# Four pieces of W1's upper blocks issued from ScalarE's queue instead of SyncE's

## The chip, the cores and the metric

The kernel runs on one core of one Trainium2 chip. The metric is the device time of one execution in microseconds (us). TensorE, VectorE, ScalarE, GpSimd and SyncE are called PE, DVE, ACT, POOL and SP where the profile does so.

## The reference, cut to what matters

Two LoRA layers with residuals are applied one after the other to an x of 8 x 256 x 1024 in float32:

```python
# layer 0: adapter chosen per sample by itok_B_0_2
x = x + (x @ W0.T + ((x @ A0[idx0]) @ B0.T) * 0.5)
# layer 1: adapter chosen per sample by itok_B_0_23
x = x + (x @ W1.T + b1 + ((x @ A1[idx1]) @ B1[idx1]) * 2.0)
```

W0 and W1 are 1024 x 1024; A0 has rank 32 and A1, B1 have rank 16.

## The kernel before, in words

Both layers are linear, so the kernel first forms a fused matrix M from (I + W0) and (I + W1), plus small fused adapters, and then multiplies the samples by M in pairs. All products of 512 x 512 blocks use seven-product schemes of the Strassen family, nested, so nearly every product needs operand sums that VectorE makes beforehand.

The order on each engine is written out by hand: the lines of the kernel body run in program order on every engine, and nothing is rescheduled. DMA transfers that SyncE and ScalarE issue share eight completion semaphores, handed round in turn; an issue that takes a semaphore over first waits for the transfer that had it before. So each of these engines' queues can wait at a DMA issue, and whatever stands behind it on that engine waits too.

The stage that the change touches is the first 45 us:

- Loads. W1 is read as four blocks of 512 x 512, block (h, i) being rows 512h to 512h+511 and columns 512i to 512i+511. `load_w1` (L163 to L171) reads a block in four pieces g = 0 to 3, each piece into 32 partitions (32g to 32g+31), in runs of 512 bytes. Block (0,0) is special: its first 256 rows come by two transfers of 128 rows each (`w1_rows`, L945, one from SP and one from ACT), and only its last 256 rows by `load_w1` (four pieces of 128 KB). Block (0,1) comes whole by `load_w1`, in four pieces of 256 KB. Both are read before the `w0n` tiles k = 4 to 7 of W0's left columns. `load_w0` (L173) reads W0 in transfers of 256 KB over all 128 partitions, in runs of 2 KB. Blocks (1,0) and (1,1) follow, then W0's right columns, then x.
- Turning. PE transposes the first rows (`turn_first`, L968, with copies by ACT and DVE at L978). `turn_w1` (L227) transposes the rest of W1 on DVE: one instruction for each k, and each needs all four pieces of its block.
- First products. `first` (L1009) multiplies tiles of I + W0 with W1's block (0,0), 26 matmuls in a row from 9.4 us on. `keep_p1` (L296, ACT) saves the results in `m22`.
- `load_a1` (L193 to L203, POOL): a one-element copy at L195 reads `m22` and so holds POOL until the first `keep_p1`. Then eight gathers of 64 KB (L198) bring the samples' adapters, and eight copies (L203) put them into the tile `a`.
- Second products. `one.products([1, 2])` and `other.products([1, 2])` (L527) read the transposes of block (0,1). After these transposes DVE makes two operand sums `z_sums` (L483), zeroes parts of banks (L646), and makes `Second.op.sums` (L418 to L421), on which the following products wait.
- `prepare_up` (L720) and `prepare_down` (L747) on PE then make the fused adapters; `prepare_down` reads the tile `a` and so waits for the last gather.

The change lies in the issuing line of `load_w1`; these lines of the body say where its first two calls stand:

```python
load_w1(wq[0, 0], 0, 0, mid, NR)      # after load_w0(0) and load_w0(1)
...
load_w1(wq[0, 1], 0, 1)               # after turn_first and first(g, k, 0) for all k
```

Of the kernel before, what the change touches and what calls it, by code (L numbers as in the profile page):

```python
# [41 lines left out]
def kernel(  # L42
# [37 lines left out]
    nc = tc.nc  # L80
# [82 lines left out]
    def load_w1(wq, h: int, i: int, lo: int = 0, hi: int = NR):  # L163

        rows = slice(h * NH + lo * SQ, h * NH + hi * SQ)
        for g in range(NG):
            cols = slice(i * NH + g * P, i * NH + (g + 1) * P)
            nc.sync.dma_start(
                wq[g * SQ : (g + 1) * SQ, lo:hi, :],
                w1[rows, cols].rearrange("(t q) c -> q t c", q=SQ),  # L170
            )  # L171
# [765 lines left out]
    with tc.manual_schedule(engines=ORDERED):  # L937
# [8 lines left out]
        for k in range(2):  # L946
            load_w0(k, 0)
        load_w1(wq[0, 0], 0, 0, mid, NR)
        for k in range(2, NB):
            load_w0(k, 0)  # L950
# [73 lines left out]
        for k in range(NB):  # L1024
# [8 lines left out]
            for g in sorted(w_groups, key=lambda g: g.m % 2 == k % 2):  # L1033
                first(g, k, 0)
        wq[0, 1] = new_w1(0, 1)
        load_w1(wq[0, 1], 0, 1)
        for k in range(NB, NK):
            load_w0(k, 0)
        load_b0()
        for i in range(2):  # L1040
            wq[1, i] = new_w1(1, i)
            load_w1(wq[1, i], 1, i)
# [330 lines left out]
```

## Time and profile before

| | |
|---|---|
| median of 3 runs | 325.2 us (324.72 to 325.85) |
| the profiled execution | 325.27 us, span of the core 323.6 us |
| PE busy | 317.1 us, 98% of the span |
| DVE busy | 253.5 us, 78% |
| ACT busy | 59.9 us, 19% |
| POOL busy | 70.0 us, 22% |
| granted PE clock | 0.999 |
| DMA | 36.42 MB, mean 113 GB/s |

A view of the profile is one of these: the page with its sections; the waits (who waited for whom, in total); the timeline (instructions in order of time: start, duration, engine, line, operation, tiles, count, and in brackets the idle time of the engine before it with what ended it); the chain of waits (the work that ended last, followed back); and a line's or tile's own rows. "SPq" is an issue by SyncE's queue, "PEld" a weight load of PE. A line named L745 is line 745 of the kernel before.

### The profile page before, as it was taken

How to read it: one execution, taken by the hardware profiler on the slowest of the kernel's cores; microseconds unless marked ns; L12 is line 12 of the kernel's file. 1: busy time of each engine (PE TensorE's matmuls, PEld its weight loads, DVE VectorE, ACT ScalarE, POOL GpSimd, SP SyncE). 2: the span in 40 equal slices, each digit the busy share in tenths (PEclk: the TensorE clock that was granted, in tenths of full speed). 3: DMA queues.
4: the chain of work that ended last, by engine and by line, in shares of the span. 5: the costliest groups of instructions: out<-in, count | busy, mean ns of one | idle time of the engine just before them, and what ended most of it. 6: DMA issues, size and time to landing. Idle time of an engine off the chain costs nothing.

```text
span 323.6 us, 4414 instructions
## 1 busy us (share of the span) xinstructions
PE 317.1 (98%) x1488; PEld 246.3 (76%) x1488; DVE 253.5 (78%) x493; ACT 59.9 (19%) x127; POOL 70.0 (22%) x107
## 2 busy tenths in 40 slices
PE   7999899999999999999999999999999999999995
PEld 6888334444588878888778888878888878888884
DVE  4789997579999999999969596939775929632965
ACT  2042215000224223540010420010240000222000
POOL 6034503455122231761004000003100000000000
PEclk9999999999999999999999999999999999999999
DMA  7999943987064994795417510335630111100113
GB/s 202 213 248 205 298 92 53 174 150 165 0 100 91 194 169 84 123 171 98 131 71 186 151 34 0 100 97 152 158 67 0 65 67 65 65 2 1 65 67 130
DMA packets 64910, 36.42 MB, mean 113 GB/s; under 512 B 45508, under 2 KB 58932, under 8 KB 64888
## 3 DMA queue, kind: packets, MB, share of 16 engines
q1 hardware_dynamic: 56088, 20.87, 29.1%
q0 software_dynamic: 8656, 15.01, 21.9%
q8 instruction: 12, 0.20, 0.2%
q10 hardware_dynamic: 144, 0.26, 0.2%
q14 instruction: 10, 0.08, 0.1%
HBM read 19.02 MB, written 8.39 MB: 85 GB/s over the span
## 4 chain that ended last, share of the span: by engine, by line
PE 88%; issue 6%; DMA 3%; POOL 2%; POOLq 1%; DVE 0%
PE bank L527 67%; PE bank L282 11%; PE bank L797 4%; PE bank L747 4%; DMA work<-in_L_cond_lora_As_dram 3%; POOLq L138 1%; PE bank L720 1%; PE bank L815 1%; POOL idx L126 0%; POOL up L993 0%; POOL down L995 0%; POOL work L198 0%; PE bank L761 0%; PE bank L547 0%; DVE work L885 0%
## 5 line engine op out<-in xcount | busy, mean ns | idle before, releaser
L509 DVE TENSOR_TENSOR work<-bank,work 128x512 f32<-128x512 f32 (+1 forms) x56 | 32.1, 620 | 30.4 <-ACT a L805 15.4
L505 ACT COPY work<-bank 128x512 f32<-128x512 f32 (+1 forms) x60 | 27.6, 547 | 77.5 <-PE bank L527 52.4
L931 POOL DMA_DIRECT2D out_dram<-work x12 | 8.9, 741 | 115.5 <-DVE work L607 115.5
L240 DVE STREAM_TRANSPOSE units<-units 128x512 f32<-128x512 f32 x32 | 20.2, 684 | 7.3 <-DMA units<-in_x_dram 7.3
L527 PE MATMUL bank<-w0n,w1T 128*128 128x256 f32 x104 | 24.1, 379 | 0.0
L527 PE MATMUL bank<-w1T,s_all 128*128 128x256 f32 x88 | 22.3, 379 | 0.0
L527 PEld LDWEIGHTS bank<-w0n,w1T 128*128 128x128 f32 x104 | 19.8, 190 | 2.7
L527 PE MATMUL bank<-w0n,m 128*128 128x256 f32 x88 | 20.9, 380 | 0.0
L527 PEld LDWEIGHTS bank<-w0n,m 128*128 128x128 f32 x88 | 16.6, 190 | 2.6 <-issue 0.4
L527 PEld LDWEIGHTS bank<-w1T,s_all 128*128 128x128 f32 x88 | 16.7, 190 | 2.3
L527 PE MATMUL bank<-tw,m 128*128 128x256 f32 x68 | 16.8, 379 | 0.0
L527 PE MATMUL bank<-tw,s_all 128*128 128x256 f32 x64 | 16.1, 379 | 0.0
L805 ACT ACTIVATE a<-bank,shift,scale 128x256 f32<-128x256 f32 x4 | 2.3, 564 | 72.4 <-PE bank L797 72.4
L227 DVE STREAM_TRANSPOSE w1T<-units 128x512 f32<-128x512 f32 (+1 forms) x16 | 14.8, 972 | 0.8 <-DMA units<-in_L_cond_W_dram 0.7
L527 PE MATMUL bank<-m,units 128*128 128x256 f32 x64 | 15.1, 379 | 0.0
L747 PE MATMUL bank<-w0n,a 128*128 128x512 f32 x32 | 14.3, 599 | 0.8 <-POOL a L203 0.8
L1009 PE MATMUL bank<-w1T,w0n 128*128 128x256 f32 x64 | 14.5, 383 | 0.4 <-DVE w1T L982 0.2
L797 PE MATMUL bank<-units,down 128*64 128x256 f32 x128 | 14.7, 382 | 0.0
L527 PE MATMUL bank<-w0n,s_all 128*128 128x256 f32 x56 | 14.4, 379 | 0.0
L527 PEld LDWEIGHTS bank<-tw,m 128*128 128x128 f32 x68 | 12.9, 190 | 1.8
L282 PE MATMUL bank<-tw,s_all 128*128 128x512 f32 x32 | 14.2, 595 | 0.0
L282 PE MATMUL bank<-w1T,s_all 128*128 128x512 f32 x32 | 14.1, 592 | 0.0
(263 smaller groups left out, 659.1 us busy)
## 6 DMA issues: line engine op xcount, KB each, us to landing
units<-in_x_dram SPq DMA_DIRECT2D x128, 64.0 KB, 2.3
out_dram<-work POOLq DMA_DIRECT2D x12, 512.0 KB, 3.4
w0n<-in_L_cond_W_dram SPq DMA_DIRECT2D x16, 256.0 KB, 8.0
units<-in_L_cond_W_dram SPq DMA_DIRECT2D x13, 256.0 KB, 8.4
out_dram<-work SPq DMA_DIRECT2D x3, 512.0 KB, 2.8
down<-in_L_cond_lora_A_dram SPq DMA_DIRECT2D x32, 32.0 KB, 2.2
w1T<-m POOLq DMA_DIRECT2D x4, 256.0 KB, 5.2
s_all<-units POOLq DMA_DIRECT2D x2, 512.0 KB, 5.3
```

What stands on the lines that cost most here:

```text
L138: return nc.values_load(fixed[0:1, b : b + 1], engines=[engine], min_val=0, max_val=n - 1, skip_runtime_bounds_check_because="clamped on t ...
L227: nc.vector.transpose(w1T[:, k, cols].rearrange("p (t q) -> p t q", q=SQ), wq[:, lo:hi].rearrange("p t (q m) -> p m t q", m=NB)[:, k % NB],)
L240: nc.vector.transpose(xT[:, NX * j : NX * (j + 1), :].rearrange("p c (t q) -> p c t q", q=SQ), xq[:, :, j, :].rearrange("p t (q c) -> p c ...
L282: nc.tensor.matmul(pm, a[:, k, :], b(k), start=first and k == 0, stop=(k == NB - 1), skip_group_check=not first,)
L505: nc.scalar.copy(at_home(v, n), whole(ps, n))
L509: nc.vector.tensor_tensor(at_home(v, n), whole(ps, n), at_home(v, n), ALU.add)
L527: nc.tensor.matmul(slot(ps, i) if dst is None else dst, lhs, rhs, start=BANK[i][0] not in started, stop=stop, skip_group_check=True,)
L720: nc.tensor.matmul(pm[g * R0 : (g + 1) * R0, :], b0[:, k, :], w1T[:, k, h * NH : (h + 1) * NH], start=(k < 4), stop=(k >= NK - 4),)
L747: nc.tensor.matmul(pm, a1[:, k].rearrange("p b r -> p (b r)"), w0n[:, k, h * NH : (h + 1) * NH], start=(k == 0), stop=(k == NK - 1),)
L797: nc.tensor.matmul(pl[n * MLOW : (n + 1) * MLOW, :], downs[n][:, k, :], x_b[f"{n + 1}{k // NB + 1}"][:, k % NB, :], start=(k == 0), stop=( ...
L931: eng.dma_start(out[b, :, h * NH : (h + 1) * NH].rearrange("(j p) d -> p j d", p=P), ob[:, 0:D].rearrange("p (j d) -> p j d", d=NH),)
L1009: nc.tensor.matmul(g.p1[:, cols], g.a[0][:, k, :], w1T[:, k, cols], start=False, stop=(k == NB - 1), skip_group_check=True,)
```

## The change

Where a block of the upper half of W1 is loaded (h = 0), pieces 1 and 3 are issued from ScalarE's queue and pieces 0 and 2 stay on SyncE's. The lower half (h = 1) stays on SyncE. Two calls have h = 0, so four of the 16 issues at this line move.

```diff
@@ -165,7 +165,8 @@
         rows = slice(h * NH + lo * SQ, h * NH + hi * SQ)
         for g in range(NG):
             cols = slice(i * NH + g * P, i * NH + (g + 1) * P)
-            nc.sync.dma_start(
+            engine = nc.scalar if h == 0 and g % 2 else nc.sync
+            engine.dma_start(
                 wq[g * SQ : (g + 1) * SQ, lo:hi, :],
                 w1[rows, cols].rearrange("(t q) c -> q t c", q=SQ),
             )
```

Lines of the changed kernel below this one have numbers higher by one.

## Prediction

> **What bounds the kernel now.** The page first: PE is busy 98% of the span at a granted clock of 0.999, so time can only come from, or go into, PE's few gaps. The change acts before 45 us, so I read the gaps there.
>
> The waits between 16 and 36 us:
>
> ```profile
> POOL work L195 <- ACT m L296: 12.9, 1, 12.9
> ...
> PEld bank L747 <- POOL a L203: 1.7, 1, 1.7
> ...
> PE bank L747 <- POOL a L203: 0.8, 1, 0.8
> DVE w1T L227 <- DMA units<-in_L_cond_W_dram: 0.7, 1, 0.7
> DVE bank L646 <- ACT bank L638: 0.5, 2, 0.3
> PEld bank L527 <- DVE s_all L419: 0.3, 1, 0.3
> ```
>
> PE's one sizeable gap is before L747, behind the last adapter gather. The 0.3 us before L527 says that DVE's sums were last there, and DVE itself waited 0.7 us for block (0,1) of W1, part of which the change moves. The chain of waits, 18 to 46 us, around that gap:
>
> ```profile
> 27.22 8.30 DMA work<-in_L_cond_lora_As_dram
> ...
> 35.58 0.30 POOL a L203
> ...
> 35.92 7.13 PE bank L747 x16
> 43.06 1.85 PE bank L720 x16
> ```
>
> The sixteen L720 matmuls take 1.85 us to the next start. The earlier sixteen start at 33.17, so PE reaches L747 at 33.17 + 1.85 = 35.02 and starts at 35.92: 0.90 us of cover for any delay that arises on PE between the first `keep_p1` (18.73, which releases the gathers) and 35. A delay before 18.73 also delays the gathers and has no cover.
>
> SP's queue, 0.5 to 14 us:
>
> ```profile
> 0.89 0.39 SPq L945 DMA_DIRECT2D units<-in_L_cond_W_dram  x1
> 1.34 0.90 SPq L176 DMA_DIRECT2D w0n<-in_L_cond_W_dram  x2
> 2.27 1.93 SPq L168 DMA_DIRECT2D units<-in_L_cond_W_dram  x4
> 4.64 0.83 SPq L176 DMA_DIRECT2D w0n<-in_L_cond_W_dram  x2
> 5.51 3.05 SPq L168 DMA_DIRECT2D units<-in_L_cond_W_dram  x4
> 8.72 3.71 SPq L176 DMA_DIRECT2D w0n<-in_L_cond_W_dram  x4
> 12.80 0.39 SPq L185 DMA_DIRECT2D b<-in_L_cond_lora_B_w_dram  x1
> ```
>
> The issue at 12.80 takes over the semaphore of piece 0 of block (0,1), issued at 5.51, so that piece had landed by 12.78: 7.3 us after its issue. And the timeline, 16 to 36 us, DVE, then PE:
>
> ```profile
> 17.07 4.10 DVE L227 STREAM_TRANSPOSE w1T<-units 128x512 f32<-128x512 f32 x4 [0.72 <-DMA units<-in_L_cond_W_dram]
> 21.09 0.38 DVE L483 TENSOR_TENSOR s_all<-w0n 128x256 f32<-128x256 f32 x1
> 21.51 0.43 DVE L483 TENSOR_TENSOR s_all<-s_all,w0n 128x256 f32<-128x256 f32 x1
> 22.10 0.27 DVE L646 MEMSET bank<- 128x256 f32 x1 [0.16 <-ACT bank L638]
> 22.70 0.27 DVE L646 MEMSET bank<- 128x256 f32 x1 [0.34 <-ACT bank L638]
> ...
> 24.34 1.99 PE L527 MATMUL bank<-s_all 128*128 128x256 f32 x8
> ```
>
> The last piece landed at 16.95 and DVE began at 17.07. DVE's waits for ACT, 0.16 + 0.34 = 0.50 us, are its slack; after them L418 and L419 run without a break and PE starts at 24.34 when they end.
>
> **The change, part by part.** *Removed from SP:* four issues of 0.43 to 0.56 us. The stage's DMA engines are busy in every slice to 36 us (digits of 9 on the page) and SP is mostly waiting for semaphores, so about 2 us of issue time saved on SP is worth nothing: what follows lands when the bytes before it have.
>
> [...]
>
> *Added to ACT, first call:* pieces 1 and 3 of block (0,0), 128 KB each, stand behind L945 and before the table load at 1.32. Two issues of 0.40 us shift the table load (1.28 us) and the dummy copy to about 3.6; ACT's next work is L978 at 5.63, after 2.79 idle, so nothing is late on ACT. But these pieces now travel beside `w0n` tile 0 instead of behind it. Tile 0 landed 3.9 us after 1.34, at 5.25, and is needed at 5.92 by L182. A 128 KB piece takes 0.7 us (pieces 1 and 2 landed at 7.99 and 8.71): shared packet by packet, half of one goes ahead, 0.35, and byte for byte a whole one, 0.7, which would be 5.95. Tile 2 landed at 10.06 against a need near 10.2; the bytes ahead of it are the same. Between 0 and 0.3 us on the uncovered path; I take 0.1.
>
> *Added to ACT, second call:* pieces 1 and 3 of block (0,1) stand behind the three L978 copies, the last of which runs from 8.33 to 8.70, and before the `keep_p1` copies. Piece 1 goes out at 8.7 instead of 7.04. Piece 3 takes over, by the new order of semaphores in the instruction streams, the one that piece 0 of the same block has. So ACT waits for piece 0 to land and piece 3 is issued then, not at 8.00. ACT is idle for 10.03 us before L296 at 18.73, so this wait hides on ACT; L296 and the gathers keep their time. What does not hide is piece 3's landing.
>
> When piece 0 lands: 12.78 if nothing runs beside it. Piece 1 reaches the DMA engines about 1.5 us after its issue (ACT's first transfer, issued at 0.89, has its first packet at 2.39), so at 10.2; piece 0's 1.45 us on the engines began near 9.7, and what is left of it, 1.0 us, doubles: 13.8. I take the middle, 13.3, as the early sharing may also mix better.
>
> [...] No row before overlaps two pieces.
>
> From piece 3's issue to its landing: no row has a 512-byte piece alone on ACT's queue. Low end: ACT's own 256 KB at L945, 0.89 to 4.62, 3.7 us, in runs of 2 KB beside one equal transfer. High end: 8.0 us, L168's median to landing. For the middle: 3.7 less the 1.36 us that two equal transfers of 0.68 take is 2.4 us of latency; piece 3's 32 packets per DMA engine then alternate with SP's, 16 of `w0n` (about 88 ns each in the trace's packets) and 16 of `b0` (28 ns), with 54 ns for each of its own: 32 x 0.054 + 16 x 0.088 + 16 x 0.028 = 3.6. Together 6.0 us. It is nearer to L945's row in queue and nearer to L168's in packets; the middle of the ends is 5.9, so 6.0.
>
> So piece 3 lands at 13.3 + 0.1 + 6.0 = 19.4 instead of 16.95: 2.45 us late. DVE's slack takes 0.50, leaving 1.95 at PE's 24.34; the cover before L747 takes 0.90, leaving 1.05. With the 0.1 from the first call: +1.15, rounded 1.2. Ends: 12.8 + 3.7 = 16.5, earlier than now, nothing lost; 13.8 + 0.1 + 8.0 = 21.9, 4.95 late, +3.55 and 0.3 more. What is late next: PE waits for nobody between L747 and 110 us. DVE, 1.95 behind, has its transposes of the lower blocks ready at 40.8 instead of 38.8 for L720 at 43.06, and W0's diagonals (L182) at 44.8 instead of 42.8 for L747's matmuls on tiles 4 to 7, 1.8 us after 44.91. One later W0 load waits for DVE's `z_sums` and goes out at about 30.1 instead of 28.19; its tile is among those that PE needs after 46. Nothing more is added for these.
>
> The profiled execution is 325.27 (323.6 plus 1.7 around), 0.07 above the median of 325.2. 325.2 + 1.2 = 326.4.
>
> **The rivals.** *Covered.* If the early sharing moves the same bytes sooner, or the piece takes under 5 us, it lands by 16.95 + 0.50 + 0.90 = 18.35 and PE's gap swallows it: 325.2, at most 0.3 more. For it: packets in runs of 512 bytes take 28 ns in the trace's packets when they first start and 50 to 57 when pieces follow one another, so mixing them with 2 KB packets may lift the rate. Against it: the DMA engines are already busy throughout.
>
> *Faster.* The mechanism is the same mixing, deciding at the last gather: if W1's and W0's queue were a microsecond ahead by 27 us, the gathers, 8.3 us from issue to landing beside it, would land sooner. The price is bounded by PE: 0.90 us before L747, and 0.31 + 0.24 more at L527 if block (0,1) also lands 0.5 earlier. It must get nearly all of this to exceed 1.0 us: 324.2. Gathers start on POOL 0.95 us apart, the last at 27.22, which speaks against so much.
>
> *Much later.* Piece 3 takes 8 us like its neighbours on SP: 325.2 + 3.6 = 328.8.
>
> That the moved issues do nothing is excluded: the streams show four of them on ACT, two behind the L978 copies.
>
> **How the numbers follow.** A measurement of this kernel can tell about 0.3% (1.0 us) from no change. Late piece (19.4, spread 18.4 to 20.9, time 325.4 to 327.9): 0.66, of which 0.19 stays under 1.0 us. Covered: 0.23. Much later: 0.05. Faster mechanism: 0.06. So slower 0.47 + 0.05 = 0.52, same 0.19 + 0.23 = 0.42, faster 0.06. The range runs from 324.8, half of the faster rival's gain, to 327.9, the late case's end, and leaves out about 1 in 10.
>
> **What would show it right or wrong.** Right: DVE's first 128x512 transpose starts near 19.5 with a wait of some 3 us on the W1 load; PE waits about 2 us at L527 (L528 after) near 22 to 26; the gap before L747 is gone, L747 starts near 37; the last gather still lands near 35.5. Wrong on the landing: the transpose starts before 18.5 and L747 near 35.9. Wrong on the cover: L747 still waits for POOL although PE is late, so the gathers moved too. Wrong on the first call: PE's L1009 run starts after 9.6 instead of 9.36.

## The result and the profile after

| | before | after |
|---|---|---|
| median of 6 runs | 325.27 us (324.72 to 325.85) | 329.26 us (327.10 to 331.69) |
| ratio | | 1.0124, interval 1.0099 to 1.0149 |
| the profiled execution | 325.27 us, span 323.6 | 329.49 us, span 327.8 |
| granted PE clock | 0.999 | 0.995 |

The changed kernel is slower by 1.2%, beyond the predicted range. Two later sets of runs of the same kernel gave smaller losses, 1.0046 (1.0024 to 1.0068) and 1.0064 (1.0042 to 1.0086), with medians of 327.6 and 327.47; the range had reached to 327.9. They are used below beside this one. A ratio is estimated from all runs of both kernels, and need not be the quotient of the two medians.

The waits between 16 and 41 us, engine and line, whom it waited for, total, times, longest:

```profile
ACT m L297 <- PE bank L1010: 10.2, 1, 10.2
DVE w1T L228 <- DMA units<-in_L_cond_W_dram: 5.6, 1, 5.6
POOL a L204 <- DMA work<-in_L_cond_lora_As_dram: 5.3, 7, 1.6
```

DVE's wait for block (0,1) is 5.6 us where it was 0.7, and PE's waits on POOL's `a` before L748 (L747 before) are no longer in the list. The gathers' landings are still waited for, but only by POOL itself. The chain, 8 to 48 us (start, duration, what), says the same from the other side:

```profile
15.12 7.71 DMA units<-in_L_cond_W_dram
...
22.88 2.03 DVE w1T L228 x2
...
24.96 13.34 PE bank L528 x52
38.30 1.85 PE bank L721 x16
40.16 7.06 PE bank L748 x16
```

Where the chain of before ran over the last gather, it now runs over the transposes of block (0,1) and PE's products. The W1 transfer that it names, issued at 15.12, is a piece of a lower block: at 22.82 only the first of its 16 shares had landed (the last at 24.04), and the transposes had begun at 21.86, right behind piece 3's landing (below). The last gather landed at 36.17 (35.53 before), 3.9 us before PE came to L748.

The issues, ScalarE's queue first, then SyncE's:

```profile
8.57 4.55 ACTq L169 DMA_DIRECT2D units<-in_L_cond_W_dram  x2
```

```profile
8.27 2.54 SPq L177 DMA_DIRECT2D w0n<-in_L_cond_W_dram  x4
11.45 0.39 SPq L186 DMA_DIRECT2D b<-in_L_cond_lora_B_w_dram  x1
```

ScalarE's two issues of block (0,1) start at 8.57, behind the last copy of L979, and take 4.55 us because the second stands there until piece 0 has landed at 12.78; it goes out at 12.80. By then SyncE has issued tiles 4 to 7 of `w0n` and `b0` (11.45). Piece 3 landed at 21.84, where the kernel before had it at 16.95. The timeline of DVE, then of PE:

```profile
21.86 4.02 DVE L228 STREAM_TRANSPOSE w1T<-units 128x512 f32<-128x512 f32 x4 [5.63 <-DMA units<-in_L_cond_W_dram]
...
27.86 0.69 DVE L420 TENSOR_TENSOR s_all<-s_all,w1T 128x512 f32<-128x512 f32 x1
```

```profile
24.96 4.71 PE L528 MATMUL bank<-w1T,w0n 128*128 128x256 f32 x12 [0.27 <-DVE w1T L228]
29.51 1.89 PE L528 MATMUL bank<-s_all 128*128 128x256 f32 x8
...
40.09 5.42 PE L748 MATMUL bank<-w0n,a 128*128 128x512 f32 x12
```

The transposes start 4.79 us later than before (21.86 against 17.07) and L748 4.17 us later (40.09 against 35.92), which is the whole loss of the span. In between, the first line of PE shows something else: twelve matmul records took 4.71 us, though the eight of the next line took 1.89. The windows (stretch, its length, then busy time and count of PE, PEld, DVE, ACT, POOL, then the granted clock, DMA share and GB/s) name it:

```profile
24.90:29.50 4.60, 4.54 (x12) 3.14 (x13) 4.48 (x10) 0.00 (x0) 3.25 (x5) 0.63 1.21 177
29.50:34.00 4.50, 4.50 (x22) 4.00 (x21) 4.47 (x11) 0.00 (x0) 1.19 (x3) 1.00 1.18 183
```

The granted clock was 0.63 on average in the first stretch and 1.00 in the second. In the clock's own records it stood at one half from 24.96 to 28.37, after 3.7 us in which PE, waiting for the transposes, had run four matmul records.

### The profile page after: what moved, and what is told of

The parts are those of the page before. It is cut to its first block, busy times and chain, and to the rows that moved or that the text cites. A ratio compares the mean times of both kernels' runs of the same rounds, so it can differ in the third digit from the quotient of the medians.

```text
span 327.8 us, 4411 instructions
## 1 busy us (share of the span) xinstructions
PE 319.1 (97%) x1488; PEld 246.6 (75%) x1488; DVE 253.9 (77%) x493; ACT 59.9 (18%) x127; POOL 69.8 (21%) x107
## 4 chain that ended last, share of the span: by engine, by line
PE 91%; DMA 6%; DVE 1%; SPq 0%; issue 0%
PE bank L528 70%; PE bank L283 11%; PE bank L798 4%; PE bank L748 4%; DMA w0n<-in_L_cond_W_dram 4%; DMA units<-in_L_cond_W_dram 2%; PE bank L721 1%; DVE w1T L228 1%; PE bank L816 1%; PE bank L762 0%; PE bank L548 0%; DVE work L886 0%; SPq L177 0%; SPq L946 0%
## 5 line engine op out<-in xcount | busy, mean ns | idle before, releaser
L528 PE MATMUL bank<-w0n,w1T 128*128 128x256 f32 x104 | 24.1, 379 | 0.0
L528 PE MATMUL bank<-w1T,s_all 128*128 128x256 f32 x88 | 22.3, 379 | 0.0
L528 PEld LDWEIGHTS bank<-w0n,w1T 128*128 128x128 f32 x104 | 19.8, 190 | 2.7
L528 PE MATMUL bank<-w0n,m 128*128 128x256 f32 x88 | 20.9, 380 | 0.0
L528 PEld LDWEIGHTS bank<-w0n,m 128*128 128x128 f32 x88 | 16.6, 190 | 2.6 <-issue 0.4
L528 PEld LDWEIGHTS bank<-w1T,s_all 128*128 128x128 f32 x88 | 16.7, 190 | 2.3
L528 PE MATMUL bank<-tw,m 128*128 128x256 f32 x68 | 16.8, 379 | 0.0
L528 PE MATMUL bank<-tw,s_all 128*128 128x256 f32 x64 | 16.1, 379 | 0.0
L1010 PE MATMUL bank<-w1T,w0n 128*128 128x256 f32 x64 | 14.7, 385 | 1.0 <-DMA w0n<-in_L_cond_W_dram 0.9
L528 PE MATMUL bank<-m,units 128*128 128x256 f32 x64 | 15.1, 379 | 0.0
L1010 PEld LDWEIGHTS bank<-w1T,w0n 128*128 128x128 f32 x64 | 12.2, 196 | 2.9 <-DVE w1T L983 1.1
L528 PE MATMUL bank<-w0n,s_all 128*128 128x256 f32 x56 | 14.4, 379 | 0.0
L748 PE MATMUL bank<-w0n,a 128*128 128x512 f32 x32 | 14.3, 599 | 0.0
L528 PEld LDWEIGHTS bank<-tw,m 128*128 128x128 f32 x68 | 12.9, 190 | 1.8
```

The lines of the kernel that those rows point to most:

```text
L528: nc.tensor.matmul(slot(ps, i) if dst is None else dst, lhs, rhs, start=BANK[i][0] not in started, stop=stop, skip_group_check=True,)
L748: nc.tensor.matmul(pm, a1[:, k].rearrange("p b r -> p (b r)"), w0n[:, k, h * NH : (h + 1) * NH], start=(k == 0), stop=(k == NK - 1),)
L1010: nc.tensor.matmul(g.p1[:, cols], g.a[0][:, k, :], w1T[:, k, cols], start=False, stop=(k == NB - 1), skip_group_check=True,)
```

## Experiments

The theory after the result: piece 3 of block (0,1) is late because of where its issue now stands, and the half clock that stands behind PE's gap (24.96 to 28.37) then slows PE's products as well. The rivals: the first call's two pieces, which go ahead of W0's tile 0; the sharing of the DMA engines by two queues, whatever the order; and the wait of piece 3 for piece 0.

**first_only**: the first call's two pieces alone on ScalarE.

```diff
-            engine = nc.scalar if h == 0 and g % 2 else nc.sync
+            engine = nc.scalar if h == 0 and i == 0 and g % 2 else nc.sync
```

> The first call alone on ScalarE: pieces 1 and 3 of block (0,0) as in the change, block (0,1) all on SyncE again. Theory of order (the DMA engines serve transfers in the order of their issue, whichever queue issued them; the loss comes from piece 3 of block (0,1) being issued at 12.8): the last piece of block (0,1) lands near 17 again; what is left is tile 0 of W0 landing some 0.9 us later, which moved keep_p1 from 18.73 to 19.08, and with it the gathers: 325.3 to 325.8. Theory of queues (a transfer on ScalarE's queue gets a poor share beside a busy SyncE queue): these two pieces were not late in the changed kernel either (landed by 8.6), so the same 325.3 to 325.8. A theory that the first call is the main loss: over 327.

Measured: 325.58 against 325.11, ratio 1.0011 (0.9994 to 1.0027). This half of the change can't be told from no change. The last piece of block (0,1) landed at 16.76, as early as before (16.95). In its profiled execution (326.50) the clock's records begin full speed only at 10.56 us (4.48 in the change), and PE's first eight products of L1010 took 3.75 us where they took 1.97 in the change, so its times aren't used for the size of the effect.

**second_only**: the second call's two pieces alone.

```diff
-            engine = nc.scalar if h == 0 and g % 2 else nc.sync
+            engine = nc.scalar if h == 0 and i == 1 and g % 2 else nc.sync
```

> The second call alone on ScalarE: pieces 1 and 3 of block (0,1) as in the change, block (0,0) all on SyncE. The semaphores now fall differently: both pieces take over semaphores of block (0,0)'s pieces, which land by 8.7, so piece 3 is no longer held for piece 0 of its own block and goes out near 9.0. Theory of order: only one or two of W0's tiles are issued ahead of the two, so the last piece lands near 18, under 1.4 us late, which the two covers take: 325.0 to 325.8. Theory of queues: 9 us on ScalarE's queue as in the changed kernel, landing after 18, but with both pieces in that queue at once up to 20: 326 to 328. A theory that any move of these pieces behind the L978 copies costs the loss: 328 to 330.

Measured: 326.46 against 325.11, ratio 1.0036 (1.0020 to 1.0053). Without the first call's issues on ScalarE, the semaphores fall differently: pieces 1 and 3 take over those of block (0,0) and go out one after the other. ScalarE's queue, then DVE:

```profile
8.96 0.88 ACTq L169 DMA_DIRECT2D units<-in_L_cond_W_dram  x2
```

```profile
18.90 4.12 DVE L228 STREAM_TRANSPOSE w1T<-units 128x512 f32<-128x512 f32 x4 [3.01 <-DMA units<-in_L_cond_W_dram]
```

Piece 3 is issued at 9.34 and lands at 18.78. L748 starts at 36.59, 0.67 us later than before. So moving the second call costs by itself, without the long wait for piece 0. The landing and the median are both later than the theory of order had said (near 18, and 325.0 to 325.8) and lie where the theory of queues had put them. What the first call adds is that it hands piece 3 that wait; hold_tile2 below asks what the wait is worth.

**sp_order**: everything on SyncE, in the order of issue that the change brings about (pieces 0 and 2, tile 4, piece 1, tiles 5 to 7, `b0`, piece 3).

`load_w1` gets an argument for the pieces that it issues; in the body:

```diff
-        load_w1(wq[0, 1], 0, 1)
-        for k in range(NB, NK):
+        load_w1(wq[0, 1], 0, 1, pieces=(0, 2))
+        load_w0(NB, 0)
+        load_w1(wq[0, 1], 0, 1, pieces=(1,))
+        for k in range(NB + 1, NK):
             load_w0(k, 0)
...
+        load_w1(wq[0, 1], 0, 1, pieces=(3,))
```

> Nothing on ScalarE; SyncE issues everything, but block (0,1) in the order in which the changed kernel issued it: pieces 0 and 2, W0 tile 4, piece 1, W0 tiles 5 to 7, b0, piece 3. Theory of order: the loss comes back without ScalarE: piece 3 lands at 20.5 to 22, the first transpose of block (0,1) starts 4 to 5 us late, 327.5 to 330. Theory of queues: the packets keep SyncE's rate, and all of these bytes were served by 20.8 before as well, so piece 3 lands at 20.8: the same sign, 327.5 to 328.5. A difference between them is in the landing: with one queue there is no waiting of ScalarE's queue, so if the queue itself costs time, piece 3 lands 1 us or more before the changed kernel's 21.84.

Measured: 327.03 against 325.11, ratio 1.0056 (1.0038 to 1.0073). ScalarE issues nothing of W1 here beyond what it did before, and a loss of 1.9 us is there, about half of the first set's 4.0 and most of what the two later sets lost (2.3 and 2.1). Piece 3 was issued at 11.67 and landed at 19.17. The clock's records of this execution begin full speed only at 10.12 us, and PE's long run of L1009 started at 11.41 (9.36 before), so that PE was late for another reason too; the comparison was made again below, on one chip with the unaltered change.

**after_filled**: the change, with five matmuls put into PE's gap, to see whether the half clock behind the gap goes, and the loss with it.

```diff
+        for n in range(5):
+            nc.tensor.matmul(
+                banks[7][:, NQ:NH],
+                ident,
+                w1T[:, 0, 0:NQ],
+                start=True,
+                stop=True,
+                skip_group_check=True,
+            )
         one.products([1, 2])
```

> The changed kernel with five extra matmuls of ident and W1 into an unused part of a bank, where PE is idle between L1009 and L527 (their results are not used). Theory that the clock gate adds to the loss: PE's granted clock, 0.63 from 24.9 to 29.5 in the changed kernel, stays at 1.0; the products before the sums no longer take 4.6 us for twelve matmul records, PE reaches the sums when DVE has them (28.6 instead of 29.5): 0.9 us less than the changed kernel's profile, median 328.0 to 328.6, and a spread under 1 us where the changed kernel had 4.6. If the clock plays no part: 329.3 with the same spread.

Measured: 327.99 against 325.11, ratio 1.007 (1.0047 to 1.0093). The clock stayed at 0.998 or more in all six runs, but the loss stayed too, and the runs spread over 1.4 us where under 1 was expected. The profiled execution can't price the clock: the clock's records begin full speed only at 10.96, PE's first products ended near 23 instead of 21.2, and the fill, from 22.90 to 25.2, stood in front of the products of L528 (started at 25.06) instead of in an idle stretch.

**after_again**: the change unaltered, beside the next three.

> The changed kernel unaltered, for its spread and a second trace. Theory of order with the clock gate on top: about 4 us over the kernel before, single runs from 327 to 331.7, the slowest of them those with a granted clock under 0.997; piece 3 of block (0,1) again issued when piece 0 lands (12.3 to 13) and landing at 19.5 to 22.

Measured: 327.60 against 325.33, ratio 1.0046 (1.0024 to 1.0068). The profiled execution was the slowest of the twelve (329.33) and repeats the first profile: piece 3 issued at 12.37 and landed at 21.40, half clock from 25.10 to 28.52, L748 at 39.93. The other eleven lie between 326.62 and 328.04 with a mean clock of 0.998 or more. So the landing came as expected, and the median's loss, 2.3 us, did not (about 4).

**piece3_back**: piece 3 of block (0,1) on SyncE again, piece 1 on ScalarE.

```diff
-            engine = nc.scalar if h == 0 and g % 2 else nc.sync
+            engine = nc.scalar if h == 0 and g % 2 and (i == 0 or g == 1) else nc.sync
```

> The changed kernel with piece 3 of block (0,1) back on SyncE; three pieces stay on ScalarE. Theory of the hold (ScalarE's wait for piece 0's semaphore, and the W0 tiles and b0 that SyncE issues meanwhile, are the loss): piece 3 goes out near 8, piece 1 on ScalarE near 8.6 is now the last and lands at 16.8 to 17.8; what stays is the first call's part: 325.2 to 326.2. Theory of queues: piece 1 takes as long on ScalarE's queue as piece 3 did and lands at 17 to 19.5: 325.5 to 327.

Measured: 325.64 against 325.33, ratio 1.0 (0.9976 to 1.0025): with piece 3 back the loss of the median is gone. Eight of the twelve runs lie between 325.06 and 325.98, four between 326.95 and 328.13. The profiled execution (327.80) is one of the four and the only one with a trace. ScalarE:

```profile
10.76 0.37 ACT L979 COPY w1T<-bank 128x256 f32<-128x256 f32 x1 [4.49 <-PE bank L969]
10.76 0.32 ACTq L169 DMA_DIRECT2D units<-in_L_cond_W_dram  x1
```

The clock's records begin full speed only at 10.69 here: PE's first products took 3.75 us instead of 1.97, its last two transposes of L969 started at 10.09 instead of 8.12, the copy of L979 waited 4.49 us for them, and piece 1, behind the copy, went out at 10.76 instead of 8.57. It landed at 20.65, and DVE's transposes started at 20.77. So piece 1, behind ScalarE's compute, took over PE's delay, 2.19 us of it at its issue; piece 3, on SyncE's queue, went out at 8.41 in the same execution.

**hold_tile2**: piece 1 of block (0,0) back on SyncE. The semaphores shift by one, and piece 3 of block (0,1) waits for W0's tile 2 instead of piece 0.

```diff
-            engine = nc.scalar if h == 0 and g % 2 else nc.sync
+            engine = nc.scalar if h == 0 and (g == 3 if i == 0 else g % 2) else nc.sync
```

> The changed kernel with piece 1 of block (0,0) back on SyncE. That rotates the semaphores by one use, so that piece 3 of block (0,1) waits on ScalarE for W0's tile 2 (landing near 10) and not for piece 0 of its own block (12.8). A middle dose: issued at 10 to 10.5 behind tiles 4 to 6 instead of behind tiles 4 to 7 and b0. Theory of order: it lands 1.4 us or so before the changed kernel's, at 18.5 to 20.5, and the time lies between: 326.5 to 328. Theory of queues: about the changed kernel's 329 if the share on ScalarE's queue sets it.

Measured: 327.40 against 325.33, ratio 1.0044 (1.0022 to 1.0067), no better than the change itself (1.0046). ScalarE's queue and DVE:

```profile
8.42 1.87 ACTq L169 DMA_DIRECT2D units<-in_L_cond_W_dram  x2
```

```profile
20.42 4.04 DVE L228 STREAM_TRANSPOSE w1T<-units 128x512 f32<-128x512 f32 x4 [4.72 <-DMA units<-in_L_cond_W_dram]
```

Piece 3 went out at 9.97, more than 2 us earlier than in the change, and landed at 20.39, only 0.2 us earlier than in the undisturbed profile of the change below (20.60). Tile 7 of `w0n`, issued on SyncE at 10.92, overtook it and landed at 19.26. An earlier landing by more than 1 us was expected and didn't come. So the wait for piece 0 isn't the price by itself: with the earlier issue the piece got ahead of `b0` alone (20.71) and still came in behind all the tiles. This is what the theory of queues had said. No run has this order of issue on SyncE alone.

**gathers_early**: the kernel before, with the marker of `load_a1` reading the transposed W1 instead of `m22`, so that the gathers don't wait for the first `keep_p1`.

```diff
-        nc.gpsimd.tensor_copy(a1_rows[0:1, 0, 0, 0:1], m22[0:1, 0, 0:1])
+        nc.gpsimd.tensor_copy(a1_rows[0:1, 0, 0, 0:1], w1T[0:1, NB - 1, NH - 1 : NH])
```

> The kernel before, all on SyncE, with one operand changed: the one-element copy that holds POOL reads the last element of W1's block (0,0) after DVE's transposes (15.7) instead of m22 after keep_p1 (18.7). The gathers start 3 us sooner, behind fewer of the lower blocks' pieces. Theory of order: served in order of issue, the last gather lands at 32 to 33.5 instead of 35.5, PE's 0.9 us before L747 goes: 324.2 to 324.8, unless the pieces of the lower blocks, now behind the gathers, make DVE late by more than 2 us, which would show as a wait before L720 or L747: 325 to 326.

Measured: 324.56 against 325.33, ratio 0.9969 (0.9947 to 0.9991), span 322.7, ahead of both kernels. The chain, 14 to 46 us:

```profile
20.76 12.41 PE bank L527 x56
33.17 1.85 PE bank L720 x16
35.02 7.07 PE bank L747 x16
```

The gathers started between 16.2 and 22.8 instead of 20.6 and 27.2, the last landed at 32.00, and L747 started at 34.96 in the timeline (35.02 in the chain), 0.96 us ahead of before; the prediction had PE arrive there at 35.02. That confirms the cover of 0.90 before L747 by taking away what PE waited for.

**after_third** and **sp_order_again**, on one chip: the change unaltered, and the same order of issue wholly on SyncE. **filled_again** repeats the fill beside them. The edits of the last two are those of sp_order and after_filled.

> The changed kernel once more, beside the next two on one chip. 2 to 4 us over the kernel before; single runs at a granted clock of 0.995 or less about 1.5 us above the rest.

> SyncE alone in the changed kernel's order of issue, beside the changed kernel on one chip. Theory of order alone: the same time as the changed kernel within 0.5 us. Theory of order plus sharing (a piece on ScalarE's queue waits as long for its first packet as any other and then shares the DMA engines with SyncE's transfers, 3.2 us where a piece alone takes 1.45): 1 to 1.5 us under the changed kernel, and piece 3 landing near 19 to 20.

> The changed kernel with five extra matmuls in PE's idle stretch, beside the changed kernel on one chip. If the clock gate costs only the runs in which it closes: no run under 0.998, no run above 329, a median within 0.6 us of the changed kernel's (the extra matmuls themselves hold the products by up to 0.3 us). If it costs every run: 0.9 us or more under the changed kernel.

Measured against 325.33: after_third 327.47, ratio 1.0064 (1.0042 to 1.0086); sp_order_again 326.72, ratio 1.0040 (1.0021 to 1.0060); filled_again 328.42, ratio 1.0092 (1.0065 to 1.0120). DVE and PE of after_third:

```profile
20.63 4.02 DVE L228 STREAM_TRANSPOSE w1T<-units 128x512 f32<-128x512 f32 x4 [5.11 <-DMA units<-in_L_cond_W_dram]
...
26.63 0.69 DVE L420 TENSOR_TENSOR s_all<-s_all,w1T 128x512 f32<-128x512 f32 x1
```

```profile
27.63 1.89 PE L528 MATMUL bank<-s_all 128*128 128x256 f32 x8
...
38.21 1.98 PE L748 MATMUL bank<-w0n,a 128*128 128x512 f32 x4
```

SyncE, DVE and PE of sp_order_again (its lines are those of before; the first line is piece 3 and the first lower piece):

```profile
12.28 1.52 SPq L168 DMA_DIRECT2D units<-in_L_cond_W_dram  x2
```

```profile
20.43 4.05 DVE L227 STREAM_TRANSPOSE w1T<-units 128x512 f32<-128x512 f32 x4 [4.58 <-DMA units<-in_L_cond_W_dram]
```

```profile
38.05 2.41 PE L747 MATMUL bank<-w0n,a 128*128 128x512 f32 x5
```

Piece 3 goes out at 12.12 from ScalarE and lands at 20.60; it goes out at 12.28 from SyncE and lands at 20.41. The products on `a` start at 38.21 and 38.05. One queue with the change's order does the same as two queues, within 0.2 us in the profiles; the medians are 0.75 us apart with intervals that overlap. So most of the loss, 1.39 of 2.14 us by the medians and nearly all of it in these two profiles (327.44 and 327.61), is in the order of issue that the change brings about. What the second queue adds is not resolved; second_only and hold_tile2, where ScalarE's pieces came in later than their order said, speak for some of it.

The fill gave no gain this time either, with the clock at 0.999 or above in its runs and one run over the 329 that was expected at most (329.91). In its profiled execution the clock's records again begin full speed late (10.11 against 5.83 in after_third), with PE at L528 at 24.88 instead of 21.82, so the cost of the half clock stays untested by the fill.

## Why the prediction was wrong

**Right: the place and the mechanism.** Piece 3 of block (0,1) waits on ScalarE for piece 0's semaphore, its landing delays the transposes, then `sums`, then PE at L747, and nothing later adds to it. Piece 0 landed at 12.78 and not at the 13.3 that was taken: piece 1's first packet came at 13.09, so they never shared the engines, and the row of before (12.78) was the better estimate. No trace has pieces 0 and 1 of this block on the engines together, so the doubling that gave 13.8 stays the author's estimate, which no run shows.

**Wrong: the term "from piece 3's issue to its landing", 6.0 us.** It was 9.04 in the first profile, 9.03 in after_again and 8.48 in after_third. The mis-sized part is the 2.4 us of latency, worked out from L945's row, where ScalarE's transfer has its first packet 1.5 us after its issue (0.89 to 2.39) and no packet of SyncE's or ScalarE's queue comes before 1.93. With the engines busy (a DMA share of 1.16 from 9.4 to 21.2 us in the first profile), ScalarE's pieces had their first packets 4.5 us (piece 1, 8.57 to 13.09) and 4.9 us (piece 3, 12.80 to 17.74) after issue. The other half, the alternating packets, was sized well: piece 3's were spread over 3.1 us (17.74 to 20.86) against 3.6. So all the rest of its 9.04 us, 5.9, stood where 2.4 was taken. The late first packet is not a trait of ScalarE's queue: counting SyncE's packets of 512 bytes in order, piece 3's begin 5.0 us after its issue in sp_order_again (12.28 to 17.32) and 5.8 in the kernel before (8.00 to 13.78).

That an empty queue starts early on busy engines was the error. The rows of before held a better estimate. SyncE's transfers there land in their order of issue (piece 0 at 12.78, 1 at 14.01, 2 at 15.50, 3 at 16.95, the tiles at 17.40, 18.08, 18.76 and 19.76, `b0` at 20.76), and between piece 3 (16.95) and `b0` (20.76) tiles 4 to 7 and `b0` take 3.81 us. The change puts those five ahead of piece 3, so its landing is to be expected at 16.95 + 3.81 = 20.76. It was 20.60 in after_third and 20.41 on SyncE alone, and 21.40 and 21.84 in the two profiles with a half clock, so this estimate is still up to 1.1 us short. The middle of two far ends was taken where counting the bytes ahead would have given the high end.

With the measured landing the rest of the sum holds. The covers were put at 0.50 + 0.90 = 1.40. In after_third the transposes are 20.63 - 17.07 = 3.56 late and L748 38.21 - 35.92 = 2.29, so the covers took 1.27. The sum on which PE's products wait, in the kernel before:

```profile
23.59 0.69 DVE L419 TENSOR_TENSOR s_all<-s_all,w1T 128x512 f32<-128x512 f32 x1
```

It ended at 24.28, and its like in after_third (L420) at 27.32, 3.04 later: DVE's slack was 0.52. The gap before L747 gave what it should, but PE's own products, held up by the transposes, put PE another 0.25 us behind the sums; the products from there to L748 took 0.10 less than before (8.73 against 8.83 to L721). The profiled time rose by 2.3 us, from 325.27 to 327.61. The first set (329.26) is nearest to the rival called much later (328.8, chance 0.05), the other two (327.6 and 327.47) to the late case's upper end (327.9). The four issues taken from SyncE took 0.33 to 0.56 us each and not 0.43 to 0.56, which changes nothing.

**Not in the sum: the clock.** In the first profile the delay of the transposes was 4.79; less 1.27 this makes 3.52, and L748 was 4.17 late. The other 0.65 can be read at the sums: PE's eight matmuls on `s_all` started 0.95 us after L420's instruction ended (28.55 to 29.51), and in after_third, at full clock, 0.31 after it (27.32 to 27.63): 0.64 more. With the clock at one half, PE's earlier products were last there, not DVE. In after_again, the other profile with a half clock, the start is 1.25 us after the sum (28.10 to 29.35), 0.94 more. The fill did not price it separately, so 0.64 and 0.94 are readings of two traces against one. The half clock lasted 3.41 us in the first profile and 3.42 in after_again, behind stretches in which PE was busy for 1.39 of 3.76 us and 1.97 of 3.70; in after_third PE was busy for 2.66 of the 4 us from 20 to 24, and the clock stayed at 1.00. What in a gap brings the half clock on, and what sets its length, these traces don't show.

**The first call** was taken at 0.1 us, by tile 0 landing at 5.95 at the latest. It landed at 6.17 against 5.25, a 0.9 us delay, and the first `keep_p1` moved by 0.35 (19.08 against 18.73). It shows no price of its own: PE came to L748 after the last gather anyway, and first_only's median shows no loss clear of noise. What it did was to hand piece 3 the semaphore of piece 0; second_only, without it, has the issue at 9.34 instead of 12.80.

**One queue or two.** The same order of issue on one queue and on two lands piece 3 (20.41 and 20.60), and starts the products on `a` (38.05 and 38.21), within 0.2 us. The move still isn't free: the measured loss was 2.1 to 4.0 us by the medians of the three sets, and the larger part of it (1.39 of 2.14 us on one chip) comes from the other place in the order that another engine's queue also means.

**What the signs showed.** The transposes started at 21.86 instead of 19.5, with a wait of 5.63 instead of 3; PE's gap before L747 was gone as foretold; L748 started at 40.09 instead of 37; the last gather landed at 36.17 instead of 35.5.

**Open:** why the first set of runs lost 1.2% and the two later ones 0.5 and 0.6%. Between the first profile and after_third, L748 differs by 1.88 us: 1.23 by the later transposes (21.86 against 20.63), the other 0.65 with the half clock. A low granted clock goes with some runs of the first set (0.988 to 0.995 in three of six), not all: 328.48 had a clock of 1.0, and there is no trace of it. The kernel before spreads too: none of its six runs beside the first set lies above 326, but 15 of the 34 beside after_again do; why is not shown.

## What to carry to other kernels

When a transfer is moved to another queue, write down the time at which each transfer is issued, sort all queues together, and count the bytes that now stand ahead of it: the piece moved here, with the DMA engines busy, landed at 20.60 to 21.84 where that order puts it at 20.76, and the empty queue bought nothing. Before moving an issue to a compute engine, look at what stands in front of it there and which semaphore it takes over: here the last copy of L979 (piece 1 went out at 8.57) and piece 0's (piece 3 went out at 12.80). If a delay leaves PE waiting, look at the granted clock behind the gap too: in two traces here it stood at one half for 3.4 us.

## What was not expected of the hardware

ScalarE's pieces were passed by neighbours on SyncE in two traces. In hold_tile2 a piece issued at 9.97 took 10.4 us while tile 7, issued at 10.92, took 8.3. In second_only a piece issued at 9.34 took 9.4 us and tile 5, issued at 9.52, 8.2. In piece3_back a piece issued at 10.76 took 9.9. In the first profile it didn't happen to piece 1 (issued at 8.57, landed at 17.05; tile 5, issued at 9.32, at 17.36). The pieces are in runs of 512 bytes and the tiles in runs of 2 KB, which no run separates from the queue.

The clock's records begin full speed at 4.48 us in the first profile and at 10.96 in after_filled, with the same instructions on PE up to there. Piece 1, which ScalarE issues behind L979's copies, moved with PE: it went out at 8.57 in the first profile and at 10.76 in piece3_back, where full speed begins at 10.69.
